# Tying VectorE's three steps of a slot to one order, and moving a held product to a free block

## The chip, the cores and the metric

The kernel runs on one core of a Trainium2 chip. The metric is the device time of one execution in microseconds (us). Before the change, three runs took 2617.64, 2617.70 and 2619.05 us; their median is 2617.7 us. The profile is of a further execution.

## The reference

Two layers run one after the other on x, of shape (2, 512, 32, 32), all in float32. The first is a deformable attention with a continuous position bias and an MLP; the second a plain attention over 1024 tokens. The stretch in question is the position bias of the first layer: for 16 groups (2 images x 8 heads), 1024 queries and 64 keys, every pair goes through a small MLP with 128 hidden channels.

```python
pos = grid_q[:, :, None, :] - grid_kv[:, None, :, :]
bias = sign(pos) * log1p(abs(pos))
bias = relu(bias @ cpb_w1 + cpb_b1)                  # 2 -> 128
bias = relu(bias @ cpb_w2 + cpb_b2)                  # 128 -> 128
bias = (bias @ cpb_w3 + cpb_b3)                      # 128 -> 1
attn = softmax(qh @ kh.T + bias)
...
h1 = gelu(xn2 @ mlp_w1.T + mlp_b1)                   # 512 -> 2048
x = x + h1 @ mlp_w2.T + mlp_b2                       # 2048 -> 512
```

## The kernel before, in words

**Slots.** The position bias is cut into 256 slots (NS): 16 groups of 16 slots (NSL), each of four keys for all 1024 queries. Channels lie on the 128 partitions. A slot s goes through these steps:

- `st_layer1(s)`, line 678: VectorE adds two tables, ta and tb, with one custom instruction and clamps below at zero; out comes a tile h1 of 128 x 4096, of which there are three buffers. Its tables serve four slots; `load_tables` brings them from DRAM over the queue of SP (line 647), `st_tables` makes them on ScalarE (lines 658 and 666).
- `st_layer2(s)`, line 695: TensorE multiplies h1 by the second layer's weights in four blocks z of 32 output channels each, one PSUM tile a block (`zp`, three buffers). ScalarE evicts each block with a relu: blocks 0 and 2 to tiles rx (line 705, three buffers), block 1 to a tile named u8, uo, uc or u4 by s % 8, block 3 to a tile ub (line 707). u4, for s % 8 = 4, has two buffers. Profile names leave digits out, so u8 and u4 both read u.
- `st_sum(s, 0)`, line 715, the first sum: VectorE adds block 0, scaled, to block 1 and so frees one rx. `st_sum(s, 2)`, the second sum, does the same with blocks 2 and 3 (it writes ub and frees the other rx), and issues a transfer on the queue of POOL that adds ub to the slot's block 1 tile (line 717).
- Folding, joining and copying on the queues of POOL (`add`, line 734) and SP (`move`, line 741) then bring the partial sums of several slots into one tile. The dictionary `due` says how many slots later each step is issued.
- `st_layer3(s)`, line 825, sums the channels with matmuls into a PSUM tile sim, one call for 16 slots. For the groups that start at slots 0 to 192 it is called 27 slots after the group's first slot, for the later ones (208, 224) 22 slots after, for 240 after the loop. In the later ones it reads the block 1 tiles of every fourth slot of the group itself: for 208 those of slots 208, 212, 216 and 220. `softmax_steps` follows as background work, and so does `later`, which prepares further groups.

**What sets the order.** The kernel is written as a program text in one order; a planner then gives every engine one fixed instruction order, by which instruction it holds to be ready first. `tc.issue_after(ins)` ties what the block issues on the engine of `ins` behind `ins` in that order and adds no wait. `newest(engine)` is the last instruction written so far for an engine. In the loop over s, lines 890 to 905, the text has the second sum of s - 1, the due steps, the table load, layer 1 of s + 2, layer 2 of s, the tables and the first sum of s; VectorE's steps are not tied.

**The first MLP unit.** `layer1` computes a quarter of the MLP's hidden layer into hm, seven blocks of 128 x 2 x 512, with a two-level fast multiplication. `twice` (lines 141 to 179) runs products for three sets at times 7 g + t, and fills at their own times in the same list. r5 and r3 are blocks 4 and 5 of hm; the third set (g = 2) writes them from time 14 on (lines 166 to 176). Block 6 is written by `spread` at the end of `layer1`. In the first unit (`early`), one plain product comes first and is kept in r3 until it is added to c11 (block 0) at 13.5; the gelu of block 0 is at 19.5 (line 1096). Other units do the product, the sum and the gelu together at 21 (`second`).

Of the kernel before, what the change touches and what calls it, by code (L numbers as in the profile page):

```python
# [57 lines left out]
def conv_seq_kernel(ctx: ExitStack, tc: tile.TileContext, x, xt, kst, pst, cst, vec, wsm, outw, w1, w2, wl, wlt, brow, out):  # L58
    nc = tc.nc
# [4 lines left out]
    def newest(engine):  # L64
        return next(i for i in reversed(nc.cur_bb.bb.instructions) if i.engine == engine)
# [70 lines left out]
    def plus(out, a, b_, op=ALU.add):  # L136
        nc.vector.tensor_tensor(out, a, b_, op)  # L137
# [69 lines left out]
    with tc.tile_pool(name="lp", bufs=2) as lp:  # L207
# [428 lines left out]

        NS = NG * NSL
        tabs, h1s, sums, sims, added = {}, {}, {}, {}, {}
        evicted, raw = {}, {}


        def load_tables(c):
            b, k, f = groups[c // 4]
            ci, kk = chain_of[b, k]
            assert ci in state
            fb = lp.tile([P, 2, W, KT], F32, name="fb", bufs=1)
            nc.sync.dma_start(
                out=fb.rearrange("p a x j -> p (a x j)"),
                in_=fdr[ci][f * len(CHAINS[ci]) + kk, c % 4].rearrange("p j -> (p j)").partition_broadcast(P),
            )  # L650
            raw[c] = fb
# [18 lines left out]
        def st_layer1(s):  # L670
            ta, tb = tabs[4 * s // KT]
            j = 4 * s % KT
            h1 = lp.tile([P, H, 4, W], F32, name="h1", bufs=3)
            a = ta[:, j : j + 4, :].rearrange("p t x -> p (t x)")
            b = tb[:, j // 4].rearrange("p y t -> p (y t)")
            step = H // 2 if s == 0 else H
            for y in range(0, H, step):
                nc.vector._custom_dve(  # L678
                    TENSOR_ADD_SAT,
                    out=h1[:, y : y + step].rearrange("p y t x -> p (y t x)"),  # L680
                    in0=a.unsqueeze(1).to_broadcast([P, step, 4 * W]),
                    in1=b[:, 4 * y : 4 * (y + step)].unsqueeze(2).to_broadcast([P, 4 * step, W]),
                    s0=FMAX, s1=0.0,
                )
            h1s[s] = h1


        def st_layer2(s):
            h1 = h1s.pop(s)
            r = []  # L690
            for z in range(4):
                ps = zp.tile([P, 2, 512], F32, name="ps2")
                for h in range(2):
                    for q in range(4):
                        nc.tensor.matmul(  # L695
                            ps[32 * q : 32 * q + 32, h, :], cw2[:, 32 * z : 32 * z + 32],
                            h1[:, 16 * h : 16 * h + 16, q, :], start=True, stop=True,
                        )
                name, bufs = (
                    ("rx", 3), (("u8", 4), ("uo", 3), ("uc", 2), ("uo", 3), ("u4", 2), ("uo", 3), ("uc", 2), ("uo", 3))[s % 8],  # L700
                    ("rx", 3), ("ub", 3),
                )[z]
                o = lp.tile([P, 2, 512], F32, name=name, bufs=bufs)
                if z % 2 == 0:
                    nc.scalar.activation(o, ps, AF.Relu, bias=sc[:, 4 + z : 5 + z])  # L705
                else:
                    nc.scalar.activation(o, ps, AF.Relu, bias=sc[:, 4 + z : 5 + z], scale=sc[:, z : z + 1])  # L707
                r.append(o)
                if z % 2 == 1:
                    evicted.setdefault(s, []).append(nc.cur_bb.bb.instructions[-1])  # L710
            sums[s] = r

        def st_sum(s, z):
            r = [t.rearrange("p h n -> p (h n)") for t in sums[s][z : z + 2]]
            nc.vector.scalar_tensor_tensor(r[1], r[0], sc[:, z : z + 1], r[1], ALU.mult, ALU.add)  # L715
            if z == 2 and s < NS - 1:
                nc.gpsimd.dma_start(out=sums[s][1], in_=sums[s][3], accum_op=ALU.add)  # L717
                added[0] = nc.cur_bb.bb.instructions[-1]
# [169 lines left out]
        st_layer1(0)  # L888
        st_layer1(1)
        for s in range(NS):  # L890
            if s > 0:
                st_sum(s - 1, 2)
            for _, go, a in sorted(due.get(s, ()), key=lambda e: e[0]):
                go(a)
            if s % 4 == 0 and s // 4 + 1 < 4 * NG:
                load_tables(s // 4 + 1)
            if s + 2 < NS:
                st_layer1(s + 2)
            st_layer2(s)


            if s % 4 == 0 and s // 4 + 1 < 4 * NG:
                with tc.issue_after(evicted[s][0]):
                    st_tables(s // 4 + 1)
            st_sum(s, 0)

            if bg is not None and (s % 4 or s < 124):
                with tc.issue_after(evicted[s][1]):
                    next(bg, None)
            if bg is not None and state.get(len(CHAINS) - 1, 0) is None:  # L910

                bg = None
                php.__exit__(None, None, None)
                opp = tc.tile_pool(name="op", bufs=1, side="right")
                op = opp.__enter__()
                op0 = op_blocks(
                    0, op.tile([P, 3, 2, 512], F32, name="op0x"), op.tile([P, 3, 2, 256], F32, name="op0w")
                )
                ready = s
            if bg is None and s > ready and (s - ready) % 4 == 0 and (s - ready) // 4 <= 8:  # L920
                i = (s - ready) // 4 - 1
                if i < 4:
                    spread(op0[1], (i,))
                else:
                    fold(nc.vector, op0[0], which=(i - 4,))

            if tails and (s % (2 if s < 60 else 4) or s >= NS - NSL):
                with tc.issue_after(evicted[s][s % 4 == 0]):
                    if next(tails[0], 0) is not None:
                        tails.pop(0)  # L930
            for t in (27, 22):
                if s % NSL == t % NSL and s >= t and (s - t < FULL) == (t == 27):
                    st_layer3(s - t)
                    tails.append(softmax_steps((s - t) // NSL))
# [37 lines left out]
    with ExitStack() as top, tc.tile_pool(name="wp", bufs=1) as wp:  # L972
# [120 lines left out]
        def layer1(p, we, w, xb, xe, hm, others=(), early=False):  # L1093
            def gelu(blk, src, scale=1.0):
                for m in range(2):
                    nc.scalar.activation(
                        hm[:, blk, m, :], src[:, m, :], AF.Gelu,
                        bias=col("mb1", 4 * p + 2 * (blk // 2) + m), scale=scale,
                    )

            c11, c12, c21, c22, r5, r3 = (hm[:, j] for j in range(6))

            def weights(q, j):
                a = FIRST_W[PARTS[q][0]]
                return [inner_w(w, we, a, a - 1)[j]]

            def moving(q, j):
                b_ = FIRST_X[PARTS[q][1]]
                return [inner_x(xb, xe, b_, b_ - 1)[j]]

            def dest(g, m, h):
                return hm[:, 2 * g : 2 * g + 2, m, 256 * h : 256 * h + 256]

            def done(g):
                if g == 0:
                    plus(c12, c12, c11)
                elif g == 1:
                    plus(c22, c22, c12)
                    plus(c21, c21, c22)
                    gelu(2, c21, -1.0)  # L1120
                else:
                    plus(c22, c22, r5)
                    gelu(3, c22, -1.0)
                    plus(c12, c12, r5)
                    plus(c12, c12, r3)
                    gelu(1, c12)

            def second():
                ps = mq.tile([P, 2, 512], F32, tag="ps2", name="sw")
                product(w, xb)(ps, 0, 0)  # L1130
                plus(c11, c11, ps)
                gelu(0, c11)

            def first():
                ps = mq.tile([P, 2, 512], F32, tag="ps2", name="sw")
                product(w, xb)(ps, 0, 0)
                nc.scalar.copy(r3, ps)

            plain = ((21, second),)
            if early:  # L1140
                plain = (-1, first), (13.5, lambda: plus(c11, c11, r3)), (19.5, lambda: gelu(0, c11))
            twice(mq, ((1, 6), (4, 7), (5, 3)), weights, moving, dest, done, (*plain, *others))
            spread([hm[:, j] for j in range(7)])

# [52 lines left out]
        for i, (b, p) in enumerate(units):  # L1197
# [10 lines left out]
            hm = cp.tile([P, 7, 2, 512], F32, tag="big", name="hm")  # L1208
# [388 lines left out]
```

## Time and profile before

| What | Value |
|---|---|
| median of three runs | 2617.7 us |
| the profiled execution | 2619.14 us |
| its span, first to last instruction | 2617.3 us |
| granted TensorE clock, mean | 0.999 |
| TensorE busy with matmuls | 2599.8 us (99% of the span) |
| VectorE busy | 2301.5 us (88%) |
| ScalarE busy | 1752.4 us (67%) |
| POOL busy | 980.2 us (37%) |
| first layer, line 678 | 257 instructions of 4404 ns |
| sums, line 715 | 1281 ns each |
| evictions, line 705 and line 707 | 1110 and 1204 ns each |

The execution took 1.8 us more than its span. In the tables and timelines, PE is TensorE, PEld its weight loads, DVE is VectorE, ACT is ScalarE; a line of a timeline gives the start, the time, the engine, the line of the code and the operation, the tile written and the tiles read, and in brackets how long the engine sat idle before and what ended that. Merged neighbours have a count. A float32 matmul is two records, so a slot's 32 matmuls are 64 records. Matmul ends are modelled, so distances of starts tell more than busy time. TensorE's matmuls of line 695 run from 38 us to 1886 us after the span's start.

### The profile page before, as it was taken

What the parts mean: (1) busy time and instruction counts of PE and PEld (TensorE: products, weight loads), DVE (VectorE), ACT (ScalarE), POOL (GpSimd) and SP (SyncE); (2) the same over time, 40 slices, a digit from 0 to 9 for tenths busy, and PEclk for the clock granted to TensorE, in tenths of its full rate; (3) what the DMA queues carried; (4) which work ended last, traced back from release to release, by engine and by line L of the source; (5) the groups of instructions that cost most, each with busy time, mean ns of one, the idle gap of its engine ahead of it and who ended that gap; (6) DMA issues with size and microseconds to landing.
All of it is one profiled execution on the core that took longest, in us unless ns stands there. A gap on an engine that the chain in (4) does not pass through costs nothing.

```text
span 2617.3 us, 48989 instructions
## 1 busy us (share of the span) xinstructions
PE 2599.8 (99%) x19660; PEld 1011.9 (39%) x19660; DVE 2301.5 (88%) x1459; ACT 1752.4 (67%) x2362; POOL 980.2 (37%) x1122
## 2 busy tenths in 40 slices
PE   9999999999999999999999999999999999999999
PEld 3332333333233233323333332332355655646556
DVE  6999999999999999999999999998776587666656
ACT  5887888888888988888788777777733242314041
POOL 1344444445444444444444444333332334200100
PEclk9999999999999999999999999999999999999999
DMA  5889999899989999899999899778777768400202
GB/s 186 174 191 193 199 195 194 191 194 190 203 187 190 188 205 198 181 191 203 190 198 192 183 193 194 169 167 182 156 202 170 149 146 169 90 16 1 73 1 56
DMA packets 177634, 428.27 MB, mean 164 GB/s; under 512 B 30048, under 2 KB 78320, under 8 KB 174720
## 3 DMA queue, kind: packets, MB, share of 16 engines
q0 software_dynamic: 107392, 273.09, 58.3%
q1 hardware_dynamic: 69584, 151.75, 17.4%
q8 instruction: 155, 2.54, 0.4%
q14 instruction: 71, 0.58, 0.1%
q10 hardware_dynamic: 432, 0.31, 0.0%
HBM read 82.16 MB, written 6.55 MB: 34 GB/s over the span
## 4 chain that ended last, share of the span: by engine, by line
PE 92%; DVE 4%; issue 2%; ACT 1%; DMA 1%; POOL 0%; DVEq 0%; ACTq 0%; POOLq 0%
PE ps L695 64%; PE sw L1077 7%; PE sw L1246 7%; PE sw L160 6%; PE sw L1024 2%; PE sw L1344 2%; PE psg L597 1%; DVE hm L137 1%; PE sim L825 1%; PE psx L1322 1%; DVE h L678 0%; DMA uc<-uc 0%; ACT rx L705 0%; PE sim L806 0%; PE pt L842 0%
## 5 line engine op out<-in xcount | busy, mean ns | idle before, releaser
L695 PE MATMUL ps<-h,cw 128*32 128x512 f32 x16384 | 1773.3, 592 | 5.2 <-ACT rx L705 3.3
L678 DVE CUSTOM_DVE_ANT_1 h<-ta,tb 128x4096 f32<-128x4096 f32 (+1 forms) x257 | 1131.6, 4404 | 25.9 <-PE ps L695 21.5
L695 PEld LDWEIGHTS ps<-h,cw 128*32 128x32 f32 x16384 | 529.7, 110 | 1216.8 <-issue 1144.1
L705 ACT ACTIVATE rx<-ps,sc 128x1024 f32<-128x1024 f32 x512 | 568.2, 1110 | 149.5 <-PE ps L695 111.5
L734 POOL DMA_DIRECT2D u<-u x397 | 409.0, 1507 | 15.1 <-DMA u<-ub 12.6
L707 ACT ACTIVATE ub<-ps,sc 128x1024 f32<-128x1024 f32 x256 | 308.3, 1204 | 87.0 <-PE ps L695 86.6
L715 DVE SCALAR_TENSOR_TENSOR ub<-rx,sc,ub 128x1024 f32<-128x1024 f32 x256 | 327.9, 1281 | 10.7 <-ACT ub L707 10.7
L717 POOL DMA_DIRECT2D uo<-ub x127 | 112.5, 886 | 589.1 <-DVE ub L715 552.0
L1077 PE MATMUL sw<-hm,w2t 128*128 128x512 f32 x448 | 194.3, 593 | 0.3 <-DVE hm L125 0.2
L707 ACT ACTIVATE uo<-ps,sc 128x1024 f32<-128x1024 f32 x128 | 154.1, 1204 | 40.0 <-PE ps L695 38.1
L715 DVE SCALAR_TENSOR_TENSOR uo<-rx,sc,uo 128x1024 f32<-128x1024 f32 x128 | 164.0, 1281 | 3.4 <-ACT uo L707 2.8
L734 POOL DMA_DIRECT2D u<-uc x126 | 126.7, 1264 | 19.1 <-DMA u<-uc 17.3
L717 POOL DMA_DIRECT2D uc<-ub x64 | 55.5, 867 | 188.1 <-DVE ub L715 154.7
L1077 PEld LDWEIGHTS sw<-hm,w2t 128*128 128x128 f32 x448 | 84.9, 190 | 104.2 <-issue 97.7
L717 POOL DMA_DIRECT2D u<-ub x64 | 54.9, 857 | 182.1 <-DVE ub L715 179.0
L137 DVE TENSOR_TENSOR hm<-hm,sw 128x512 f32<-128x512 f32 x79 | 57.6, 732 | 74.1 <-PE sw L160 51.1
L734 POOL DMA_DIRECT2D uc<-uc x63 | 106.3, 1687 | 2.3 <-DMA uc<-ub 2.3
L734 POOL DMA_DIRECT2D uc<-uo x63 | 102.8, 1632 | 10.8 <-DMA uc<-uo 10.4
L1410 POOL DMA_DIRECT2D xs<-rs x6 | 7.2, 1200 | 259.1 <-DVE rs L137 259.1
L707 ACT ACTIVATE u<-ps,sc 128x1024 f32<-128x1024 f32 x64 | 77.1, 1204 | 24.5 <-PE ps L695 20.8
L658 ACT ACTIVATE ta<-fb,vs 128x512 f32<-128x512 f32 (+1 forms) x65 | 89.0, 1373 | 5.8 <-DMA fb<-fdr 5.8
L707 ACT ACTIVATE uc<-ps,sc 128x1024 f32<-128x1024 f32 x64 | 77.0, 1203 | 21.6 <-PE ps L695 18.4
(297 smaller groups left out, 2644.9 us busy)
## 6 DMA issues: line engine op xcount, KB each, us to landing
uo<-ub POOLq DMA_DIRECT2D x127, 512.0 KB, 5.4
fb<-fdr SPq DMA_DIRECT2D x64, 512.0 KB, 5.8
u<-ub POOLq DMA_DIRECT2D x64, 512.0 KB, 6.5
uc<-ub POOLq DMA_DIRECT2D x64, 512.0 KB, 6.1
u<-u POOLq DMA_DIRECT2D x63, 256.0 KB, 7.0
u<-uo SPq DMA_DIRECT2D x63, 256.0 KB, 5.8
u<-uo POOLq DMA_DIRECT2D x63, 256.0 KB, 7.3
uc<-uc POOLq DMA_DIRECT2D x63, 256.0 KB, 8.1
```

The costliest lines, as they stand in the source:

```text
L137: nc.vector.tensor_tensor(out, a, b_, op)
L160: nc.tensor.matmul(bank[:, e, :], w, x, start=(q in (1, 2, 5) and e == k == 0), stop=True, skip_group_check=True,)
L658: nc.scalar.activation(ta.rearrange("p j x -> p x j")[:, :, j0:j1], fb[:, 0, :, j0:j1], AF.Identity, bias=col("cb1"), scale=col("w1x"),)
L678: nc.vector._custom_dve(TENSOR_ADD_SAT, out=h1[:, y : y + step].rearrange("p y t x -> p (y t x)"), in0=a.unsqueeze(1).to_broadcast([P, ste ...
L695: nc.tensor.matmul(ps[32 * q : 32 * q + 32, h, :], cw2[:, 32 * z : 32 * z + 32], h1[:, 16 * h : 16 * h + 16, q, :], start=True, stop=True,)
L705: nc.scalar.activation(o, ps, AF.Relu, bias=sc[:, 4 + z : 5 + z])
L707: nc.scalar.activation(o, ps, AF.Relu, bias=sc[:, 4 + z : 5 + z], scale=sc[:, z : z + 1])
L715: nc.vector.scalar_tensor_tensor(r[1], r[0], sc[:, z : z + 1], r[1], ALU.mult, ALU.add)
L717: nc.gpsimd.dma_start(out=sums[s][1], in_=sums[s][3], accum_op=ALU.add)
L734: nc.gpsimd.dma_start(out=out, in_=in_, accum_op=ALU.add)
L1077: nc.tensor.matmul(ps[:, m, :], w[:, a, k, m * P : (m + 1) * P], x[:, b_, k, :], start=(k == 0), stop=(k == 1),)
L1246: nc.tensor.matmul(ps[:, m, :], w[:, a, k, c + m * P : c + (m + 1) * P], x[b_][:, k, :], start=(k == 0), stop=(k == nk - 1),)
```

## The change

It does two things. In the loop, layer 1 of s + 2 is written first, and the three steps on VectorE are tied in a chain: layer 1 of s + 2 behind the first sum of s - 1, the second sum of s - 1 behind that layer 1, the first sum of s behind that second sum. In the first MLP unit, the held product goes to block 6 of hm, which nothing else uses before the final `spread`, and its sum and gelu come together at 21.

```diff
-        evicted, raw = {}, {}
+        evicted, raw, summed = {}, {}, []
...
         for s in range(NS):
+            if s + 2 < NS:
+                with tc.issue_after(summed[-1]) if summed else nullcontext():
+                    st_layer1(s + 2)
+                    summed.append(newest(mybir.EngineType.DVE))
             if s > 0:
-                st_sum(s - 1, 2)
+                with tc.issue_after(summed[-1]):
+                    st_sum(s - 1, 2)
+                    summed.append(newest(mybir.EngineType.DVE))
             for _, go, a in sorted(due.get(s, ()), key=lambda e: e[0]):
                 go(a)
             if s % 4 == 0 and s // 4 + 1 < 4 * NG:
                 load_tables(s // 4 + 1)
-            if s + 2 < NS:
-                st_layer1(s + 2)
             st_layer2(s)
...
-            st_sum(s, 0)
+            with tc.issue_after(summed[-1]):
+                st_sum(s, 0)
+            summed.append(newest(mybir.EngineType.DVE))
...
-                nc.scalar.copy(r3, ps)
-
-            plain = ((21, second),)
-            if early:
-                plain = (-1, first), (13.5, lambda: plus(c11, c11, r3)), (19.5, lambda: gelu(0, c11))
+                nc.scalar.copy(hm[:, 6], ps)
+
+            def merge():
+                plus(c11, c11, hm[:, 6])
+                gelu(0, c11)
+
+            plain = ((-1, first), (21, merge)) if early else ((21, second),)
```

## The prediction

> **What bounds the kernel now.** I read the page's chain first, then the timelines of VectorE (DVE) and TensorE (PE) wherever VectorE's order differs from the tied one.
>
> ```profile
> PE 92%; DVE 4%; issue 2%; ACT 1%; DMA 1%; POOL 0%; DVEq 0%; ACTq 0%; POOLq 0%
> ...
> L695 PE MATMUL ps<-h,cw 128*32 128x512 f32 x16384 | 1773.3, 592 | 5.2 <-ACT rx L705 3.3
> ```
>
> TensorE carries 92% of the chain. From the starts of L695's matmuls: four run at once, a group every 0.43 us, 16 groups or 6.87 us a slot; 256 slots are 1759 of the 1847 us from 38 to 1886 us. The other matmuls between them take 82, and pauses with no other matmul 6.0, of which 3.7 lie between 1805 and 1829 us. After 1886 us pauses over 0.1 us sum to about 6, the longest 1.33. So little is there to win. VectorE's slot costs 4.34 + 1.20 + 1.20 = 6.74 us (distances of starts), only 0.13 less than TensorE's: once late, it hardly catches up.
>
> Numbering the instructions of L678 and L715 by slot (L first layer, A first sum, B second), VectorE already runs L(s+2), B(s-1), A(s) in 232 of its 253 or so turns. Others are slots 0 to 3, 228 to 239 and 244 to 255. Here is slot 228:
>
> ```profile
> 1680.56 4.43 DVE L678 CUSTOM_DVE_ANT_1 h<-ta,tb 128x4096 f32<-128x4096 f32 x1
> 1684.90 1.28 DVE L715 SCALAR_TENSOR_TENSOR ub<-rx,sc,ub 128x1024 f32<-128x1024 f32 x1
> 1688.58 4.43 DVE L678 CUSTOM_DVE_ANT_1 h<-ta,tb 128x4096 f32<-128x4096 f32 x1 [2.40 <-PE ps L695]
> 1692.92 1.28 DVE L715 SCALAR_TENSOR_TENSOR ub<-rx,sc,ub 128x1024 f32<-128x1024 f32 x1
> 1694.12 1.28 DVE L715 SCALAR_TENSOR_TENSOR uo<-rx,sc,uo 128x1024 f32<-128x1024 f32 x1
> ...
> 1705.55 1.28 DVE L715 SCALAR_TENSOR_TENSOR u<-rx,sc,u 128x1024 f32<-128x1024 f32 x1 [0.41 <-ACT u L707]
> 1707.35 8.76 DVE L678 CUSTOM_DVE_ANT_1 h<-ta,tb 128x4096 f32<-128x4096 f32 x2 [0.52 <-ACT tb L666]
> ```
>
> After L230 and B227 the sum A228 (it writes u) is missing; it comes 21 us later, behind L231, B228, A229, B229, A230 and B230. TensorE and ScalarE (ACT) say why:
>
> ```profile
> 1702.36 1.90 PE L825 MATMUL sim<-u,w3f 128*32 128x512 f32 x16
> ...
> 1704.31 1.20 ACT L707 ACTIVATE u<-ps,sc 128x1024 f32<-128x1024 f32 x1 [0.50 <-PE sim L825]
> ```
>
> Tag u4 has two buffers, so slot 228 takes slot 212's, and layer 3 of the group from slot 208 (L825) still reads that one until slot 230. Slot 244 meets slot 228's buffer in the same way:
>
> ```profile
> 1806.02 3.64 PE L695 MATMUL ps<-h,cw 128*32 128x512 f32 x32 [0.41 <-ACT rx L705]
> 1811.56 7.07 PE L695 MATMUL ps<-h,cw 128*32 128x512 f32 x64 [1.89 <-ACT rx L705]
> 1818.56 1.09 PE L806 MATMUL sim<-qa,kz 64*64 64x512 f32 x8
> 1819.58 1.92 PE L825 MATMUL sim<-u,w3f 128*32 128x512 f32 x16
> 1821.32 7.05 PE L695 MATMUL ps<-h,cw 128*32 128x512 f32 x64
> 1829.07 3.21 PE L695 MATMUL ps<-h,cw 128*32 128x512 f32 x28 [0.69 <-DVE h L678]
> ```
>
> So the odd order is the planner's way round a real wait. In the first MLP unit a wait is plain:
>
> ```profile
> 1958.09 1.03 PE L160 MATMUL sw<-xe,w1x 128*128 128x256 f32 x4
> 1960.28 1.99 PE L160 MATMUL sw<-xe,w1e 128*128 128x256 f32 x8 [1.16 <-ACT hm L166]
> ```
>
> The copy of L166 overwrites part of r3, which the sum of 1958.23 (1.22 us, L137) still reads.
>
> [...] L231 waited 2.40 us for TensorE and nothing passed it. So what is tied behind A228 waits with it. [...] here a 128 KB accumulating transfer needed 6.7 us from issue to landing, and I use that.
>
> **The change, part by part.** It adds and removes no engine instruction in the slots; ties are order alone. In the program's text B(s-1), with its POOL transfer, falls behind L(s+2), and L comes ahead of the due joins and SP's table load; L issues nothing on POOL or SP, so these queues keep their order. Slots 4 to 227 keep their order: nothing. In slots 0 to 3, L2 comes ahead of A0: A0 starts at 43.19, the wait of L2 for its buffer (gs, to DRAM) ended at 43.8, so A0 ends near 49.4; slot 1's second rx eviction, which needs its buffer, is at 52.44. Nothing; up to 1 if cover is missing.
>
> Slot 228. The order is L230, B227, A228, L231, B228, A229, L232. A228 waits for ScalarE's eviction of u, this for L825, this for the joins on POOL (DMA issue at 1688.29 and 1688.82, u<-uc, landing 6.7 later: 1695.5). Behind A228 in VectorE's queue stand L231 (TensorE needs it for slot 231) and B228 and A229, which free rx buffers: three exist, held by 228's two and 229's first, so ScalarE can't take slot 229's third block, and with u's block two of three PSUM buffers are stuck. TensorE runs dry in the first block of slot 230. B228's POOL transfer is behind it too; L825 needs only older sums. At the earliest: L825 1696 to 1697.8, u evicted by 1699.0, A228 until 1700.2, L231 until 1704.6, B228 1705.8, A229 1707.0, L232 1711.3. I replay the blocks by hand from the trace's durations (1.72 us a block on TensorE, evictions 1.0 and 1.1): slot 230's first block at 1697.8, its second in u's PSUM buffer at 1699.5, its third when A228's rx has let slot 229's block out (1701.3); its first block itself leaves only with B228's rx (1706.8), so slot 231 starts at 1706.7 and 232 at 1713.7; at 1715.9 if L825 stands behind slot 230's first block. The same replay with the order of before gives 1711.5 for 232; the timeline shows 1711.92. So **+2.2 to +4.4**, bounds 0 and +5; I take **+3.0**.
>
> Until 244, L(k) then ends only 2 to 3 us ahead of slot k. Shown is B239 at 1776.6, 5.2 ahead of slot 242 (1795.56 - 2 x 6.87 = 1781.8); with 2 us, it and the joins behind it come about 3.3 later relative to TensorE. Side work there is small (L851 0.68, L852 0.17) and covered by those 2 to 3 us: 0.
>
> Slot 244. The join was issued at 1807.84 and landed 5.8 later, 1813.6. The same replay: L825 ends 1815.8, A244 at 1817.0, L247 until 1822.6, slot 248 at 1831.7, against 1829.07 shown: +2.6. With the 3.3 of the joins, +5.9. Below: the shown order loses 3.7 here, because B244 stood behind L247; an earlier L825 could give 1.5 of it back. **Bounds -1.5 and +8; I take +4.5.**
>
> The end. L254 would end about 3 us before slot 254 (1872.15 shown), so B251 comes at 1869.2 and not 1861.28, 8 us later; from its POOL transfer (1864.04) to the landing that L825 of the last group awaited (1886.9) the shown chain takes 23 us. Cover is the first projection, 56 matmul records by 0.43 or 24 us of L1024, which the planner can put ahead. **+0.3**; without cover up to +4, taken as 2 at most.
>
> MLP unit. The product goes to hm[:, 6], written by nothing else before the unit's last spread; L166 no longer waits: -1.33, the pause from 1958.74. The merged sum and gelu have VectorE idle at 1960.9 to 1963.2 (2.23 before L137) and gelu is read only after 1963.9. **-1.3**; 0 if gelu comes late, since layer 2's first matmuls then wait.
>
> Sum: 3.0 + 4.5 + 0.3 - 1.3 = **+6.5**. The profiled execution took 2619.14 (span 2617.3, the rest around it): 2625.6. It lies 1.4 over the median 2617.7 of the runs; on the median, **2624.2**, +0.25%.
>
> **Rivals.**
> Covered hold: the planner moves L825 up to 1695.5 and TensorE fills the hold with it. For it: slot 231 starts only about 0.6 later by L231, and shown pauses are small. Against: rx and PSUM. 0.6 + 0.6 - 1.3 = -0.1: 2617.6.
> Pauses removed (faster): in slots 244 to 248, B244 no longer behind L247 gives back 3.7, slot 228 0.3, the MLP 1.3, the last L825's 0.9: -6.2, 2611.5. It decides so only if u4's old buffer is free when A228's turn comes, that is L825 over by about 1686 where its joins are issued at 1688.8. Much against it.
> Hold feeds itself: late sums delay the joins that the next release needs by a slot more (6.9) in 244 and the end: +14, 2632.
> No effect: the tied order is the shown one except at those slots, so a plan that stays is the first rival's number.
>
> **How the numbers follow.** My case 0.52 (own range 2619 to 2631; four fifths of it beyond 2622.9), covered hold 0.27, pauses removed 0.12, hold feeds itself 0.09. A measurement of this kernel can tell about 0.2% or 5.2 us from no change. Slower: 0.42 + 0.09 = 0.51; within: 0.10 + 0.27 = 0.37; faster 0.12. The lower bounds sum to 0 - 1.5 + 0 - 1.3 = -2.8, 2614.9; the upper to 5 + 8 + 2 + 0 = +15, 2632.7. Range 2614.5 to 2633, which leaves out the faster rival and a tail of the last.
>
> **What would show it.** A228 directly after B227, idle 10 us or more for ACT u, and L231 behind it; TensorE's pause before L825 at slot 230 and again at 246, 2 to 6 us each; A and B then in the tied order to slot 255; in the MLP, no pause before the L160 of 1960. Wrong would be: idle of VectorE there without a TensorE pause (covered hold), L825 ahead of slot 229 (pauses removed), or changes in slots 4 to 227.

## The result and the profile after

The changed kernel takes 2631.44 us (median of 6 runs, 2630.52 to 2633.16), the kernel before 2617.97 in the same comparison (6 runs): a ratio of 1.0051, 95% interval 1.0039 to 1.0064, or 13.5 us more. The forecast was 2624.2, +6.5. The profiled execution took 2630.66 with a span of 2628.9; that of before lay 1.2 over its median and this one 0.8 under, so the two traces show only 11.5 of the 13.5 us. Those 11.5 are placed below. The ratios of the experiments lie up to 0.001 under those of the medians, as in those rounds 18 to 36% of the runs of the kernel before took 2621 to 2626 us.

The page's chain and the costliest group, for the changed kernel:

```profile
PE 92%; DVE 4%; issue 2%; ACT 1%; DMA 1%; POOL 0%; DVEq 0%; SPq 0%; ACTq 0%; POOLq 0%
...
L695 PE MATMUL ps<-h,cw 128*32 128x512 f32 x16384 | 1775.0, 592 | 9.7 <-ACT rx L705 3.5
```

TensorE is the bound as before; its idle time ahead of L695 grew from 5.2 to 9.7 us. The shares say no more than that. VectorE's timeline at slot 228 (start, duration, engine, line, idle time before it and what ended it):

```profile
1700.91 1.28 DVE L715 SCALAR_TENSOR_TENSOR u<-rx,sc,u 128x1024 f32<-128x1024 f32 x1 [14.60 <-ACT u L707]
1702.12 4.42 DVE L678 CUSTOM_DVE_ANT_1 h<-ta,tb 128x4096 f32<-128x4096 f32 x1
1706.45 1.28 DVE L715 SCALAR_TENSOR_TENSOR ub<-rx,sc,ub 128x1024 f32<-128x1024 f32 x1
1707.65 1.28 DVE L715 SCALAR_TENSOR_TENSOR uo<-rx,sc,uo 128x1024 f32<-128x1024 f32 x1
```

A228 stands directly behind B227 and holds the queue for 14.60 us; L231, B228 and A229 follow it without a gap, as late as the wait made them. TensorE meanwhile:

```profile
1695.34 1.88 PE L825 MATMUL sim<-u,w3f 128*32 128x512 f32 x10
1696.86 2.08 PE L695 MATMUL ps<-h,cw 128*32 128x512 f32 x16
1698.60 1.03 PE L825 MATMUL sim<-u,w3f 128*32 128x512 f32 x6
1700.93 1.92 PE L695 MATMUL ps<-h,cw 128*32 128x512 f32 x16 [1.30 <-ACT u L707]
1703.67 3.64 PE L695 MATMUL ps<-h,cw 128*32 128x512 f32 x32 [0.81 <-ACT rx L705]
...
1708.63 7.07 PE L695 MATMUL ps<-h,cw 128*32 128x512 f32 x64 [0.32 <-ACT ub L707]
```

The planner did move layer 3 (L825) up, from 1702.36 to 1695.34, as the covered hold had it. It was not enough: the pauses that follow end with ScalarE's evictions of u, rx and ub. Slot 244 has the same picture: A244 waits 11.34 us, and TensorE has pauses of 1.29, 0.82 and 1.33. The end is new. TensorE, then POOL's transfers, of the changed kernel:

```profile
1887.52 7.07 PE L695 MATMUL ps<-h,cw 128*32 128x512 f32 x64 [1.00 <-ACT uc L707]
1899.22 1.34 PE L825 MATMUL sim<-u,w3f 128*32 128x512 f32 x4 [4.62 <-issue]
```
```profile
1889.09 0.84 POOL L734 DMA_DIRECT2D uc<-uo  x1 [5.93 <-DMA uc<-uo]
1896.57 0.82 POOL L734 DMA_DIRECT2D u<-uc  x1 [4.89 <-DMA u<-uc]
```

The same two steps in the kernel before:

```profile
1884.28 0.82 POOL L734 DMA_DIRECT2D u<-uc  x1 [5.00 <-DMA u<-uc]
```
```profile
1886.92 1.05 PE L825 MATMUL sim<-u,w3f 128*32 128x512 f32 x4 [0.70 <-issue]
```

Layer 3 of the last group waits 4.62 us. "issue" names no releaser, but the last of its joins on POOL is issued at 1896.57 and lands at 1899.13, 0.09 us before layer 3 starts; before, it is issued at 1884.28 and lands at 1886.83, again 0.09 before. Join and layer 3 are both 12.3 us late. B251, which starts this chain, came at 1873.98 and not at 1861.28.

The offset of TensorE's matmuls, after minus before, gives the whole account: +0.15 up to slot 229; +5.3 at slot 234; +4.5 at 246; +8.4 at 255; +13.7 at the end of the last group's layer 3; +13.1 when the first MLP unit's second layer starts; +11.6 at 2197 us, and +11.5 from then to the end.

### The profile page after: what moved, and what is told of

Read it like the earlier page. It is cut to its first block, busy times and chain, and to the rows that moved or that the text cites. A ratio compares the mean times of both kernels' runs of the same rounds, so it can differ in the third digit from the quotient of the medians.

```text
span 2628.9 us, 48993 instructions
## 1 busy us (share of the span) xinstructions
PE 2604.4 (99%) x19660; PEld 1010.0 (38%) x19660; DVE 2298.4 (87%) x1459; ACT 1750.9 (67%) x2362; POOL 982.3 (37%) x1122
## 4 chain that ended last, share of the span: by engine, by line
PE 92%; DVE 4%; issue 2%; ACT 1%; DMA 1%; POOL 0%; DVEq 0%; SPq 0%; ACTq 0%; POOLq 0%
PE ps L695 63%; PE sw L1083 7%; PE sw L160 7%; PE sw L1254 7%; PE sw L1030 2%; PE sw L1352 2%; PE psg L597 1%; PE sim L825 1%; PE psx L1330 1%; DVE hm L137 0%; DVE ub L715 0%; DVE h L678 0%; DMA u<-uc 0%; ACT ub L707 0%; PE sim L806 0%
## 5 line engine op out<-in xcount | busy, mean ns | idle before, releaser
L695 PE MATMUL ps<-h,cw 128*32 128x512 f32 x16384 | 1775.0, 592 | 9.7 <-ACT rx L705 3.5
L678 DVE CUSTOM_DVE_ANT_1 h<-ta,tb 128x4096 f32<-128x4096 f32 (+1 forms) x257 | 1130.4, 4399 | 23.2 <-PE ps L695 18.7
L695 PEld LDWEIGHTS ps<-h,cw 128*32 128x32 f32 x16384 | 526.7, 110 | 1225.0 <-issue 1133.5
L715 DVE SCALAR_TENSOR_TENSOR u<-rx,sc,u 128x1024 f32<-128x1024 f32 x64 | 81.7, 1276 | 30.2 <-ACT u L707 30.1
L734 POOL DMA_DIRECT2D uc<-uo x63 | 101.8, 1616 | 12.3 <-DMA uc<-uo 11.3
L707 ACT ACTIVATE u<-ps,sc 128x1024 f32<-128x1024 f32 x64 | 77.0, 1204 | 30.5 <-PE ps L695 21.3
L734 POOL DMA_DIRECT2D u<-uo x63 | 85.3, 1354 | 25.8 <-DMA u<-uo 20.3
```

The lines of the kernel that those rows point to most:

```text
L678: nc.vector._custom_dve(TENSOR_ADD_SAT, out=h1[:, y : y + step].rearrange("p y t x -> p (y t x)"), in0=a.unsqueeze(1).to_broadcast([P, ste ...
L695: nc.tensor.matmul(ps[32 * q : 32 * q + 32, h, :], cw2[:, 32 * z : 32 * z + 32], h1[:, 16 * h : 16 * h + 16, q, :], start=True, stop=True,)
L734: nc.gpsimd.dma_start(out=out, in_=in_, accum_op=ALU.add)
```

## The experiments

Each kernel was timed in five rounds beside the kernel before, whose medians were 2618.5 to 2618.6. "Over before" is the difference of those medians. Tied order means L(s+2), B(s-1), A(s).

### The two parts apart

Ties alone, and the held product alone. The edit of the first, against the changed kernel, begins so (the second is the kernel before with the other half of the change):

```diff
-                nc.scalar.copy(hm[:, 6], ps)
...
+                nc.scalar.copy(r3, ps)
```

> Ties on VectorE as in the change, the MLP unit as before. My theory (the tied sums of slots 228 and 244 hold VectorE's queue while the buffer of tag u4 is still read by layer 3, and the lost lead makes the last layer 3 late): the whole of the +13 is here, so 13 to 15 us over the kernel before, with the pauses before slots 231, 232 and 248 and before L825 of the last group as in the changed kernel. Rival (the held product and its merged gelu cost time that the slots don't show): clearly under +12.

2632.55 us, +14.1 over before, ratio 1.0050 (1.0037 to 1.0062). The rival falls: the whole loss is in the ties.

> The held product in hm alone, VectorE's order free. My forecast said -1.3. From the profile of the changed kernel, where the pause of 1.33 is gone but new ones of 0.28 and 0.38 us stand in the same unit: -0.3 in the unit, and up to -1.5 more later if the shift of the later MLP units belongs to this part: -1.8 to -0.3. Rival (the hm part costs): +0.5 or more.

2617.62 us, -0.9, ratio 0.9996 (0.9988 to 1.0005), so not told from nothing. In the trace of this kernel TensorE's offset against the kernel before shrinks by 0.7 over the unit (from +0.8 to +0.1), and the pause by L166 is gone.

### The wait taken away

Slot 228's tile gets a buffer of tag u8, which is free by then; slot 244's u4 then follows slot 220's:

```diff
-                    ("rx", 3), (("u8", 4), ("uo", 3), ...)[s % 8],
+                    ("rx", 3), ("u8", 4) if s == 228 else (("u8", 4), ("uo", 3), ...)[s % 8],
```

With ties:

> The changed kernel with slot 228's tile taken from tag u8 instead of u4, so that neither slot 228 nor slot 244 has to wait for layer 3's reads; the tie stays. My theory: VectorE's idle time of 14 and 11 us and the pauses of TensorE go, and so does the lateness of the end: 2611 to 2619, i.e. 12 us or more under the changed kernel. Rival (the tied order itself costs, through the joins that come later or the lead that is shorter): within 4 us of the changed kernel, 2627 to 2632.

And without, in the kernel before:

> The kernel before with the same change of tag and nothing else. If the planner's odd order after slot 228 is its way round that buffer alone, VectorE's order becomes the tied one without any tie, and the pauses of 3.7 us between 1805 and 1829 and the smaller ones go: 2612 to 2616. Rival (those pauses come from elsewhere, as from joins or from ScalarE): within 1 us of the kernel before, 2617 to 2619.

2613.51 us (0.9975, 0.9966 to 0.9985) and 2612.85 (0.9974, 0.9964 to 0.9983): -5.0 and -5.6, both in the ranges of my theory. With the ties kept, 18 us of the changed kernel's time are gone. VectorE and TensorE with ties:

```profile
1686.41 1.28 DVE L715 SCALAR_TENSOR_TENSOR u<-rx,sc,u 128x1024 f32<-128x1024 f32 x1 [0.21 <-ACT u L707]
```
```profile
1681.46 20.81 PE L695 MATMUL ps<-h,cw 128*32 128x512 f32 x192
1702.09 1.90 PE L825 MATMUL sim<-u,w3f 128*32 128x512 f32 x16
1703.80 7.05 PE L695 MATMUL ps<-h,cw 128*32 128x512 f32 x64
```

A228 comes 14.5 us earlier, and TensorE runs through, with layer 3 back where it was in the kernel before. From 1600 us to the MLP it has no pause over 0.12. So the tied order costs nothing that can be told by itself (the same kernel without ties, run last below, takes 2612.86); it costs where one of its steps has to wait. And the kernel without ties comes to the tied order by itself once the tile is free (its trace has L230, B227, A228, L231 from 1681.16 on): its odd order was the planner's way round this buffer, and freeing the buffer is worth 5.6 us.

### One hold at a time

A hold is VectorE's idle time in front of A228 or A244. Only slot 244 from u8 (228 holds), and both from u8, where 244 follows slot 224's tile, read by the same layer 3, and 228 follows slot 200's:

> The changed kernel with only slot 244's tile taken from tag u8 (slot 216's buffer, free since slot 230): the hold at slot 228 stays, the one at 244 goes. My theory: +5 at slots 230 to 232 as in the changed kernel, the pauses near slot 246 gone (worth about 9 against the changed kernel's slots 244 to 255), and the end in between: 2617 to 2622. Rival (each hold costs nothing alone, it's the second that costs because the lead was lost at the first): like the kernel without holds, 2613.5 to 2615.

> The changed kernel with slots 228 and 244 both from tag u8: slot 228 then has slot 196's or an older buffer and doesn't wait, slot 244 has slot 224's, which the same layer 3 reads that it waits for in the changed kernel. So only the hold at 244 is left. My theory: 4 to 6 us at slots 246 to 249 as in the changed kernel, and a part or all of the end's 5: 2618 to 2624, TensorE level with the kernel without holds up to slot 245. Rival (second hold costs only because of the first): 2613.5 to 2615.

2621.18 us (1.0007, 1.0001 to 1.0014) and 2625.25 (1.0027, 1.0016 to 1.0038): +2.7 and +6.7 over before, 7.7 and 11.7 over the tied kernel without holds. The first lies in the range of my theory, the second 1.3 above it; both rivals fall. Against that kernel's matmuls, slot 255 is late by 5.9 us with the hold at 228 alone, by 5.7 with the one at 244 alone, and by 12.7 with both: the holds add up, nearly. What the one at 228 costs (5.6 at slot 232) isn't given back in the 23 slots that follow: in the tied kernel without holds TensorE has no pause over 0.12 us there that could take it up. VectorE, with 0.13 us to spare in a slot (6.74 of 6.87), is late for long: with the hold at 228 alone it runs from 1701 us without a pause until this one, near slot 251:

```profile
1857.40 1.28 DVE L715 SCALAR_TENSOR_TENSOR uo<-rx,sc,uo 128x1024 f32<-128x1024 f32 x1 [0.21 <-ACT uo L707]
```

The end does not add: what comes to the lateness of slot 255 by the start of the last layer 3 is 2.6, 5.2 and 4.8.

### What is ahead of the waiting sum

First the chain of ties passes A228 and A244 by, and the planner puts each one turn later, behind L231, B228 and A229 (and their like at 244):

```diff
+            if s in (228, 244):
                 st_sum(s, 0)
...
+            else:
...
```

> The changed kernel in which the first sums of slots 228 and 244 alone aren't tied, and the chain of ties passes them by; buffers as in the changed kernel. The planner then puts each behind the next slot's first sum, and first layer and sums of slot 229 and 245 no longer stand behind the wait. My theory (it is what stands behind the two sums in the queue that costs): 2614 to 2621, no pause over 1 us near slots 230 and 246. Rival (the late tile itself costs, through the joins and layer 3 that follow it, or through ScalarE's queue): 2625 or more.

2627.15 us (1.0031, 1.0019 to 1.0044), +8.6. My number was wrong, and the rival's range came true:

```profile
1705.82 1.28 DVE L715 SCALAR_TENSOR_TENSOR u<-rx,sc,u 128x1024 f32<-128x1024 f32 x1 [10.15 <-ACT u L707]
1707.62 4.42 DVE L678 CUSTOM_DVE_ANT_1 h<-ta,tb 128x4096 f32<-128x4096 f32 x1 [0.52 <-ACT tb L666]
1711.96 1.28 DVE L715 SCALAR_TENSOR_TENSOR ub<-rx,sc,ub 128x1024 f32<-128x1024 f32 x1
```

I had counted on layer 3 at 1695; with this order the planner leaves it at 1702.63, so the hold is 10.15 us with other steps behind it (L232, then B229 at 1711.96). But A228 runs at 1705.82, as in the kernel before (1705.55), which is only 0.5 us behind the kernel without holds at slot 232 where this one is 5.4 behind. So a late tile alone isn't what costs, though the rival's number was the better one.

Then one step is exchanged: L231 ahead of A228, L247 ahead of A244, all tied, and the two sums left out at their old place:

```diff
+            if s in (229, 245):
+                with tc.issue_after(summed[-1]):
+                    st_sum(s - 1, 0)
...
+            if s not in (228, 244):
...
```

> The changed kernel with one step of the tied order exchanged at the two slots: L231 stands ahead of A228, and L247 ahead of A244; the second sum of the slot and the next first sum (B228, A229 and B244, A245) still stand behind the waiting sum. My theory (TensorE starves because these sums free no rx buffer, so that ScalarE can't empty PSUM; the first layer isn't the late one, since TensorE's pauses there end with ScalarE's evictions and none with L678): within 2 us of the changed kernel, 2629 to 2632. Rival (the first layer behind the wait is what TensorE lacks): the two holds' pauses shrink, 2619 to 2625.

2620.13 us (1.0002, 0.9993 to 1.0010), +1.6 over before, which can't be told from nothing. 12 of the 13.5 us are gone, and my expectation, that this exchange changes little, falls. The rival's number holds, with a correction to its mechanism. VectorE and TensorE:

```profile
1689.88 4.42 DVE L678 CUSTOM_DVE_ANT_1 h<-ta,tb 128x4096 f32<-128x4096 f32 x1 [2.41 <-PE ps L695]
1702.07 1.29 DVE L715 SCALAR_TENSOR_TENSOR u<-rx,sc,u 128x1024 f32<-128x1024 f32 x1 [7.76 <-ACT u L707]
1703.27 1.28 DVE L715 SCALAR_TENSOR_TENSOR ub<-rx,sc,ub 128x1024 f32<-128x1024 f32 x1
```
```profile
1702.09 1.92 PE L695 MATMUL ps<-h,cw 128*32 128x512 f32 x16 [1.30 <-ACT u L707]
1704.82 10.51 PE L695 MATMUL ps<-h,cw 128*32 128x512 f32 x96 [0.81 <-ACT rx L705]
```

The two first pauses are the ones of the changed kernel (1.30 and 0.81), at 228 and at 244: these belong to the late eviction of u and to rx. What is gone is all that followed them: the pauses by ub and rx at slots 231, 232 and 247, and most of the end's (0.35 is left). In neither kernel does a pause here end with L678, so TensorE didn't lack the first layer's tile. It was VectorE's time: 4.34 us of work done inside the hold, not behind it, so that B228 comes 1.2 us after A228 and not 5.5, and every later sum that much nearer its due. The rx buffers are still how this reaches TensorE. ScalarE's evictions of slot 230's first and third block, in the changed kernel and in this one:

```profile
1708.48 2.11 ACT L705 ACTIVATE rx<-ps,sc 128x1024 f32<-128x1024 f32 x2
```
```profile
1705.76 2.21 ACT L705 ACTIVATE rx<-ps,sc 128x1024 f32<-128x1024 f32 x2
```

They need the rx tiles that B228 and A229 free. B228 ends at 1707.73 in the changed kernel and at 1704.55 here. I had overlooked that these sums, though still behind A228, come earlier.

Last, B228 and B244 ahead too:

> As the kernel with L231 ahead of A228 and L247 ahead of A244, but with B228 and B244 ahead of them too; only A229 and A245 of the steps in question still stand behind. The theory after the earlier runs: what counts is how much VectorE time is lost idle at the hold, i.e. the end of the wait less the end of what stands ahead of it. B228 moves 1.2 us into the hold, but layer 3 now stands half a slot later in TensorE's order (between the second and fourth block of slot 230), which puts the end of the hold 1.5 to 3 us later: no gain, 2619 to 2624. Rival (every step taken ahead of the sum gains, since it frees an rx buffer earlier): 2614 to 2618.

2637.02 us (1.0064, 1.0052 to 1.0076), +18.4, far outside both. VectorE and POOL:

```profile
1710.35 1.28 DVE L715 SCALAR_TENSOR_TENSOR u<-rx,sc,u 128x1024 f32<-128x1024 f32 x1 [16.07 <-DMA u<-ub]
```
```profile
1704.84 0.85 POOL L717 DMA_DIRECT2D u<-ub  x1 [12.72 <-ACT u L707]
```

I had overlooked that B228 issues a transfer into the same tile. Written ahead of A228, it makes the sum wait for its landing, 5.8 us beyond the end of u's eviction (1704.55). So this run doesn't test what it was for; it shows what a longer hold (16.1 us at both slots) does.

In the four kernels with both holds, the time goes with the length of the two holds together: 16.9 us (first layer ahead), 21.3 (sums untied), 25.9 (the changed kernel) and 32.2 (second sum ahead too), and 6.6, 13.6, 17.9 and 23.5 us over the tied kernel without holds. That fits the account by VectorE's time; it doesn't prove it, since these kernels also differ in which steps stand behind the wait.

### The end

The first projection's first two products are written ahead of the last layer 3, and this is tied behind them:

```diff
+        for p in (1, 2):
...
+                    nc.tensor.matmul(
...
+        with tc.issue_after(newest(mybir.EngineType.PE)):
+            st_layer3(NS - NSL)
```

> The changed kernel with the first two products of the first projection (16 matmul records, 6.9 us) written ahead of the last group's layer 3 and layer 3 tied behind them on TensorE. My forecast counted on the planner to put that work there; it did not, and TensorE waited 4.8 us. My theory: the work was free to go there, and the wait is covered: 4 to 5.5 us under the changed kernel, 2626 to 2627.5. Rival (the projection can't start there, or layer 3 and the softmax after it set the end, so that what is gained there is lost behind it): 2630 to 2633.

2628.86 us (1.0039, 1.0027 to 1.0052), 2.6 less than the changed kernel's 2631.44, between the two forecasts:

```profile
1893.96 7.13 PE L948 MATMUL sw<-qa,vp 128*128 128x512 f32 x16
1901.02 1.05 PE L825 MATMUL sim<-u,w3f 128*32 128x512 f32 x4
...
1907.17 0.66 PE L842 MATMUL pt<-ident,ss 128*128 128x128 f32 x4 [0.81 <-ACT ss L838]
1908.61 7.10 PE L1041 MATMUL sw<-op0x,op0w 128*128 128x512 f32 x16 [0.78 <-issue]
```

The projection was free to start at 1893.96, and covers the wait. But the products that were ahead are missing behind layer 3, where the softmax now has TensorE wait: pauses of 0.97, 0.95, 0.37 and 1.04 at L842, L1041, L877 and again L1041 (by distances of starts; the idle times in brackets are smaller, as ends are modelled). Against the changed kernel, and counted from slot 255, TensorE is 4.8 us ahead at the first L1041, 3.1 after the last of these pauses, and 1.9 at the end; the rest goes in the MLP units, and why is open. The ties of the last slots are not what makes layer 3 late: the tied kernel without holds has them too, and there layer 3 follows slot 255 without a pause (1881.68).

### Both gains together, and the gelu

> The kernel before with slot 228's tile from tag u8 and the held product in hm, no ties: the two parts that gained alone. If they add up (2612.9 with the tag alone, -0.9 for the held product alone): 2611.5 to 2612.5. If the held product moves the later units instead, 2613 to 2614, as with ties.

2612.86 us (0.9970, 0.9959 to 0.9981), between the two forecasts: nothing on top of the tag alone (2612.85). Then, with `issue_after(newest(mybir.EngineType.Activation))` around the merged gelu:

> The same kernel with the merged gelu of the first MLP unit tied behind the copies that were issued before it on ScalarE, so that the loading of the table (1.28 us) and the gelu no longer stand ahead of L170's copy. My theory (the new pauses of 0.29 and 0.37 us in that unit are from this): both go, 0.3 to 0.7 us less than without this tie. Rival (the gelu then comes late for layer 2's first matmuls, and the pause moves there): the same or up to 1.5 us more.

2613.23 us (0.9970, 0.9958 to 0.9981). The pause of 0.37 is gone, and ones of 0.85 and 0.19 stand behind it (by distances of starts); that of 0.29 stays. The rival holds. The best kernel here is 2612.9 us, 18.6 less than the changed one.

## Why the forecast was right in kind and short in size

By the terms of the sum, in the traces (forecast, then measured):

- **Slots 0 to 227**: 0; 0.15.
- **Slot 228**: +3.0; +5.1 (the 5.3 at slot 234 less this 0.15). Who waits for whom was right: VectorE's idle time (14.60 us), what stands behind it, and TensorE's pauses, though these come behind layer 3's pieces and not before them. Layer 3 came in two pieces and ended at 1699.63, not 1697.8; so A228 ended at 1702.2 and not 1700.2, and slot 231 started at 1708.63 and not 1706.7. The replay missed that layer 3 in two pieces costs about 0.7 more between starts, that the lateness goes on (pauses of 0.32 by ub and 0.60 by rx, at the start of slots 231 and 232), and 0.9 for four matmuls of L806 that now come here; in the kernel before all eight come at 1818.56.
- **Slots 234 to 255**: 0 up to slot 244 and then +4.5; +3.1. Right in size, as the difference of two larger terms. Against the tied kernel without holds, the second hold costs 6.9 us (12.7 at slot 255 less 5.8 at 234); the detour of the kernel before, which is saved here, is worth 3.8 in the same stretch. My 2.6 + 3.3 less up to 1.5 had both in it, the cost too low and the saving too, so that the size came out is in part luck.
- **The end**: +0.3; +5.3. **This is the step that failed**: the cover of the wait. The forecast said "Cover is the first projection, 56 matmul records by 0.43 or 24 us of L1024, which the planner can put ahead." B251 was indeed late (12.7 us; I had 8), and the cover was there, as the run with the projection first shows. But the planner kept layer 3 ahead, and even a cover made by hand gained only 2.6 us, since the softmax behind layer 3 then has TensorE wait. The bound "without cover up to +4" was nearly the right figure for the pause (4.6); I had cut it to 2.
- **MLP unit**: -1.3; -0.6. The pause of 1.33 went. In its place the table load and gelu stand ahead of the copy of L170:

```profile
1973.47 1.28 ACT L1102 ACT_TABLE_LOAD   x1
1974.76 0.72 ACT L1102 ACTIVATE hm<-hm,vs 128x512 f32<-128x512 f32 x1
1975.39 0.57 ACT L170 COPY hm<-sw 128x512 f32<-128x512 f32 x1
```

  with pauses of 0.28 and 0.38 by distances of starts (the second ends with that copy). Before, the same two stood ahead of it (1960.24 and 1961.54, the copy at 1962.16), but the load began as TensorE's pause ended (1960.28), and no pause ended with that copy.
- **Later units**: not forecast; -1.5. Pauses of 0.88, 0.45 and 0.26 near 2096, 2143 and 2197 shrank or went. In the same stretch the trace of the ties alone has -0.9, that of the held product alone -1.5, that of the free u8 alone +0.5. What sets it is open, and I don't count it as a gain.

The sum is 11.6, against +6.5. The end alone is 5.0 of the 5.1 that are missing; that the other misses (+2.1, -1.4, +0.7, -1.5 and 0.15) cancel is luck. Within slot 228 the replay had L231 ahead of B228 and the rx buffers behind that, as the trace shows; what it did not say is that the 4.3 us of the first layer could have been done during the hold. How the rest divides between u's eviction and rx stays open: a fourth rx buffer wasn't tried.

Of the rivals, "hold feeds itself" (2632, chance 0.09) came nearest in number. Its account fits the end, where late joins delay layer 3, but not slot 244: there the joins were issued 5.2 us later than before (1812.51 against 1807.31), as late as the matmuls and not a slot more, and the second wait is the shorter one. "Pauses removed" (2611.5) had named its condition, that u4's old buffer be free; the kernels that free it take 2613.5 and 2612.9.

## What to carry to other kernels

A tie cost nothing here that can be told while the step tied was ready (2613.5 us with ties, 2612.9 without). A step that had to wait for a buffer turned the tie into idle time (14.60 and 11.34 us), and VectorE, busy for 98% of a slot (6.74 of 6.87 us), needed more than twenty slots to catch up (with the hold at 228 alone, until slot 251); what TensorE, the bound engine, had lost by then stayed lost (5.6 us at slot 232, 5.9 at 255). Before tying an order, look at why the free order differs: here one buffer explained it, and freeing the buffer gained more (5.6 us) than any order did. If the wait must stay, try the longest ready step ahead of it (here 12 of 13.5 us), but check what that step issues: a transfer into the waiting step's own tile made the wait longer (by 5.8 us beyond the end of u's eviction, to 16.07 us). And cover that a planner "can" use counts only if the trace shows it used.

## What was not expected of the hardware

Switching ScalarE's function table in the middle of work took 1.28 us in the changed kernel: the eviction of L176 ahead of the load ended at 1973.45, the load started at 1973.47 and took 1.28, and the gelu started at 1974.76. All 20 loads in that trace took 1.28 us, and of the other 19, 17 have the next instruction start 0.01 us behind them. The forecast for the MLP unit had no term for this load, which stands ahead of L170's copy there.
